# Four graph layers in fp32 on one core: VectorE and block transfers for a transpose, RMS factors by way of DRAM, bias rows on VectorE, five graphs in flight

## The chip, the cores and the metric

The kernel runs on one core of a Trainium2 chip. The time is that of one execution on the device, in microseconds. A core has five engines that work side by side, each through its own queue in order: TensorE (PE: matmuls and transposes, results into PSUM), VectorE (DVE) and ScalarE (ACT) for elementwise work, GpSimd (POOL), and SyncE (SP), which issues the DMA transfers. An instruction that needs another engine's result waits for a semaphore, and all behind it in its queue waits too.

## The reference

There are 32 graphs of 512 nodes with 256 features and a dense 512x512 adjacency matrix each. Four graph layers follow each other, each as `x = layernorm(x + layer(x, adj))`, all in float32:

```python
# layer 0: two-layer perceptron on (1 + eps) x + adj x
h = relu(((1 + eps) * x + adj @ x) @ W1 + b1)           # 256 -> 512
y = h @ W2 + b2                                          # 512 -> 256
# layer 1: linear, aggregate, leaky
y = prelu(adj @ (x @ W.T + b), alpha)
# layer 2: norm, aggregate, two weights, residual
h = layer_norm(x)
y = x + relu((adj @ h) @ W_rel + b_rel + h @ W_root)
# layer 3: aggregate, RMS norm over 1024 hidden features, silu
h = (eps * x + adj @ x) @ W1 + b1                        # 256 -> 1024
h = silu(h * rsqrt(mean(h * h, -1) + 1e-6) * w)
y = h @ W2 + b2                                          # 1024 -> 256
```

## The kernel before

The 32 graphs pass through the core as a pipeline. A graph's nodes are laid over 128 partitions in 4 chunks, so a token-major activation is a tile of 128 x 4 x 256; feature-major ones are 128 features by 512 nodes a chunk. Every matrix product is done by a seven-product scheme on 2x2 blocks (`seven`, with the sums of blocks in `left_sums` and `right_sums`): fewer matmuls on TensorE, more additions on VectorE.

The order of the instructions is worked out in Python while the kernel is built. `Plan` (line 191) records each operation with the engines that may do it (its "ways"), a duration for each way, and what it reads and writes. `Plan.order` (line 317) then goes through a modelled time: each engine takes, among the operations that can start, the one with the best rank, where the rank holds the graph's number times a period plus the time by which TensorE will need the result. `best` (line 311) tries each of `RULES` (line 95) and keeps the order that ends first. A DMA in this model costs SP `ISSUE` = 0.45 us and ends `ADVANCE` + size/385 + `AFTER` later (line 76). What comes out is one fixed sequence for each engine.

Memory is handed out in the same pass. A `Pool` has tiles, a `Room` is one tile's use. There are 36 rooms of 128 x 1024 floats, 12 small tiles and 8 PSUM banks (line 444 and on); at most `FLIGHT` = 4 graphs are open at a time. A younger graph must leave some tiles spare for the older ones.

The parts that the change touches, per graph:

- `Adjacency` (line 634) loads the adjacency in four pieces, forms its block sums (`sums`, line 650), and keeps a plain copy of four diagonal strips (two chunks of 128x128 each) in a room of its own, by four tile-to-tile transfers (`carry`); layer 0 adds (1 + eps) to the diagonals (`with_loops`, line 671), `restore` (line 667) copies the four strips back before layer 1, and layer 3 adds its eps to them.
- `plus_row` (line 874) adds a bias row to a token-major activation in layers 0 and 3: four GpSimd instructions of 128x256.
- `layer2` (line 935) needs its input h feature-major, as hT. For each of two chunks TensorE transposes four squares of 128x128 into a PSUM bank (`flip`), and ScalarE or VectorE copies the bank to a room. Then VectorE forms differences of hT's halves (`dense_sums`), and TensorE multiplies.
- `layer3` (line 955) sums the squares of the hidden features into `acc`; `column_sums` (line 793) adds over the features by a VectorE reduction that transposes 32x32 blocks, three small additions and four small steps `ts` (one for each 32 partitions); GpSimd raises to the power -1/2 (`inv_sqrt`); TensorE spreads the 512 factors over all partitions by four transposes of a broadcast column into a PSUM bank `pr`; VectorE multiplies hT by `pr`, ScalarE applies silu, and the last product follows.
- `load_x` and the output are one transfer each.

Nearly all instructions are recorded through one helper, so the profile shows them under line 266 (compute) and line 280 (DMA). One finds them by the names of their tiles: room (working tiles), ps (PSUM), few (small tiles), ident (the identity for transposes).

Of the kernel before, what the change touches and what calls it, by code (L numbers as in the profile page):

```python
# [26 lines left out]


def in_psum(x):
    return isinstance(x, Part) and x.room.pool.psum  # L30
# [35 lines left out]
def gpsimd_time(n):  # L66
    return 0.15 + n * 0.0024, 0.05


# [6 lines left out]
ISSUE, ADVANCE, AFTER, LANES = 0.45, 1.5, 0.35, 8  # L76
# [18 lines left out]
RULES = [(50, 2, last, near) for last in (12, 20) for near in (0, 0.5, 1)]  # L95


class Pool:


    def __init__(self, tiles, grain, spare, psum):
        self.tiles, self.grain, self.spare, self.psum = tiles, grain, spare, psum
        self.clear()

    def clear(self):
        self.rooms = [None] * len(self.tiles)

    def free(self):

        return sorted(  # L110
            (0.0 if r is None else r.until, i)
            for i, r in enumerate(self.rooms)
            if r is None or not r.left
        )


class Room:


    def __init__(self, pool):  # L120
        self.pool = pool
        self.uses = 0
        self.clear()

    def clear(self):
        self.index = None
        self.left = self.uses
        self.until = 0.0


class Part:
# [34 lines left out]
    def place(self):  # L166
        v = self.room.pool.tiles[self.room.index]
        for step in self.steps:
            v = step(v)
        return v  # L170
# [3 lines left out]
class Op:  # L174

    graph: int
    rank: tuple
    ways: dict  # L180
    port: set
# [9 lines left out]
class Plan:  # L191
# [10 lines left out]
    def grains(self, x):  # L202
        part = isinstance(x, Part)
# [4 lines left out]
        for step, n in dims[:-1]:  # L208
            starts = [s + step * i for s in starts for i in range(n)] if step else starts
        step, n = dims[-1]  # L210
        return {
            (key, g)
            for s in starts
            for g in range(s // grain, (s + step * (n - 1)) // grain + 1)
        }

    def add(self, ways, out, ins, ordered=None, port=(), kbytes=0):
        me = len(self.ops)
        op = Op(self.graph, (self.graph, me), ways, port, "scalar" in ways, kbytes)
        self.ops.append(op)  # L220
        before, results = set(), set()
        writes = self.grains(out) if out is not None else set()
# [22 lines left out]
    def do(self, out, *ways, ordered=None, scrap=None):  # L245
# [3 lines left out]
        port = set()  # L249
        for e, method, _, args, kw in ways:  # L250
            tiles = [x for x in (*args, *kw.values()) if isinstance(x, (bass.AP, Part))]
            ins += tiles
            if e == "gpsimd" and kw.get("op") != ALU.pow or e == "vector" and not (
                method.startswith("bn_") or any(in_psum(x) for x in tiles)
            ):
                port.add(e)

        def issue(engine, method, args, kw):
# [14 lines left out]
            out, ins, ordered, port,  # L273
        )

    def move(self, out, src, kbytes, inward=True):


        def issue():
            self.nc.sync.dma_start(*(x.place() if isinstance(x, Part) else x for x in (out, src)))  # L280

        self.add(
            {"sync": ((ISSUE, ADVANCE + wire_time(kbytes) + AFTER), issue)},
            out if inward else None, [src] if isinstance(src, Part) else [], kbytes=kbytes,
        )
# [31 lines left out]
    def order(self, period, pace, last, near):  # L317
# [15 lines left out]
        oldest, port, wire, lanes = 0, 0.0, 0.0, [0.0] * LANES  # L333
        can_start = {i for i, n in enumerate(behind) if not n}
        done = []
        while can_start:
# [4 lines left out]
            def rooms_free(op):  # L341

                count = {}
                for r in op.rooms:
                    if r.index is None:
                        count[r.pool] = count.get(r.pool, 0) + 1
                at = 0.0
                for pool, n in count.items():
                    if pool not in room_at:
                        room_at[pool] = pool.free()  # L350
                    n += pool.spare[min(op.graph - oldest, len(pool.spare) - 1)]
                    if op.graph - oldest >= self.flight or n > len(room_at[pool]):
                        return None
                    at = max(at, room_at[pool][n - 1][0])
# [3 lines left out]
            for i in can_start:  # L358
# [4 lines left out]
                if op.kbytes:  # L363
                    wait = max(wait, lanes[0])
                at = {
                    e: max(free[e], wait, ready[i][e], port if e in op.port else 0.0)
                    for e in op.ways
                }
                way = min(at, key=lambda e: at[e] + sum(op.ways[e][0]) + (YIELD if op.yields and e == "vector" else 0.0))
# [11 lines left out]
            if op.kbytes:  # L381
                wire = max(wire, t + ADVANCE) + wire_time(op.kbytes)
                end = wire + AFTER
                lanes = [*lanes[1:], end]
            if engine in op.port:
                port = end
            for r in op.rooms:
                if r.index is None:
                    r.index = r.pool.free()[0][1]
                    r.pool.rooms[r.index] = r  # L390
# [16 lines left out]
def tile_gnn_stack(ctx: ExitStack, tc: tile.TileContext, a: dict, out: bass.AP):  # L407
# [36 lines left out]
    FLIGHT, ROOMS, SMALL = 4, 36, 12  # L444
# [3 lines left out]
    psum = ctx.enter_context(tc.tile_pool(name="psum", bufs=1, space=bass.MemoryType.PSUM))  # L448
    plan = Plan(nc, FLIGHT)

    def pool(kind, name, n, size, grain, spare):
        return Pool(
            [kind.tile([P, size], F32, tag=f"{name}{i}", name=f"{name}{i}") for i in range(n)],
            grain, spare, kind is psum,
# [3 lines left out]
    rooms = pool(work, "room", ROOMS, NC * D, P, (0, 4, 6, 8))  # L458
# [5 lines left out]

    def gpsimd(method, n, *args, **kw):
        return "gpsimd", method, gpsimd_time(n), args, kw
# [22 lines left out]
    def both(method, o, x, y, engines):  # L489
        plan.do(o, *(e(method, span(o), x, y) for e in engines))  # L490

    def add(o, x, y, *engines):
        both("tensor_add", o, x, y, engines or (vector,))

    def sub(o, x, y, *engines):
        both("tensor_sub", o, x, y, engines or (vector,))

    def mul(o, x, y):
        both("tensor_mul", o, x, y, (vector,))
# [10 lines left out]
    def carry(o, x):  # L510
        plan.move(o, x, P * span(o) / 256)

    def inv_sqrt(o, x):
        n = span(o)
        plan.do(
            o, ("gpsimd", "tensor_tensor", power_time(n), (x, mhalf[:, 0:n]), dict(op=ALU.pow))
# [3 lines left out]
    def room(*shape):  # L520
        return Part(Room(rooms)).shaped(*shape)

# [54 lines left out]
    mhalf = constant("mhalf", [P, 2 * NC])  # L577
# [56 lines left out]
    class Adjacency:  # L634
# [15 lines left out]
        def sums(self):  # L650
# [8 lines left out]
            kept = room(4, HC, P)  # L659
            self.plain = [kept[:, i] for i in range(4)]  # L660
            for d, o in zip(self.plain, self.loops):
                if plan.graph:
                    carry(d, o)
                else:
                    copy(d, o)

        def restore(self):
            for d, o in zip(self.plain, self.loops):
                carry(o, d)

        def with_loops(self, loop):
            for d, o in zip(self.plain, self.loops):
                add(o, d, loop.unsqueeze(1).to_broadcast(list(o.shape)), vector)

        def row_sums(self):

            rows = room(N)
# [79 lines left out]
    def dense_sums(upper, lower):  # L757
# [3 lines left out]
        for pairs in zip(upper, lower):  # L761
            blocks = [x[:, :, j * TH : (j + 1) * TH] for x in pairs for j in range(2)]
            sums = right_sums(*blocks, [room(2, TH) for _ in range(3)], blocks[1])
# [29 lines left out]
    def column_sums(t, put):  # L793
# [3 lines left out]
        few = small(16)  # L797
# [7 lines left out]
        for q in range(1, P // Q):  # L805
            add(few[0:Q], few[0:Q], few[q * Q : (q + 1) * Q])
        for q in range(P // Q):
            put(slice(q * Q, (q + 1) * Q), few[0:Q, q :: P // Q])
# [64 lines left out]

    def plus_row(x, r):

        for c in range(NC):
            add(x[:, c, :], x[:, c, :], r, gpsimd)
# [31 lines left out]
    def layer1(x, adjacency):  # L909
# [4 lines left out]
        column_sums(rows, lambda p, sums: ts(rs[p], sums, 1.0, None, ALU.mult))  # L914
# [20 lines left out]
    def layer2(h, xx, u, adjacency):  # L935

        aT = aggregate(h, adjacency)
        hT = Wide(DC)
        for j in range(DC):
            ps = bank(N)  # L940
            for c in range(NC):
# [144 lines left out]
```

## Time and profile before

| | us |
|---|---|
| median of 3 runs (2363.84 to 2365.42) | 2364.99 |
| the profiled execution | 2366.02 |
| its span, first to last instruction | 2364.2 |

The mean granted TensorE clock in it was 0.997. In a line of groups stand the source line, engine, operation, tiles written and read, shapes and count, then the busy time in us and the mean of one instruction in ns, then the engine's idle time just before and what ended it. A float32 matmul has two rows on TensorE (MATMUL on PE, its weight load on PEld), a transpose one. What matters for the change, per graph of the 32, from the groups by form:

| what | count a graph | mean of one, ns |
|---|---|---|
| PE transposes of h (ident, room) | 8 | 273 |
| PE transposes of the factors (ident, few) | 4 | 274 |
| ACT copies of hT out of PSUM, 128x512 | 2 | 597 |
| POOL bias adds, 128x256 | 8 | 769 |
| POOL power, 128x4 | 4 | 1243 |
| DVE products of hT with pr, 128x512 | 8 | 679 |
| DMA tile to tile, 128 KB, issue to landing | 8 | 2.2 us |

The durations of PE rows overlap, so the time that one costs is the distance between starts in a row of equal ones. A line of the stretches has its borders, its length, and the busy time and instruction count of PE, PEld, DVE, ACT and POOL, then the granted clock, the share of the DMA engines and their GB/s.

### The profile page before, as it was taken

What the parts mean: (1) busy time and instruction counts of PE and PEld (TensorE: products, weight loads), DVE (VectorE), ACT (ScalarE), POOL (GpSimd) and SP (SyncE); (2) the same over time, 40 slices, a digit from 0 to 9 for tenths busy, and PEclk for the clock granted to TensorE, in tenths of its full rate; (3) what the DMA queues carried; (4) which work ended last, traced back from release to release, by engine and by line L of the source; (5) the groups of instructions that cost most, each with busy time, mean ns of one, the idle gap of its engine ahead of it and who ended that gap; (6) DMA issues with size and microseconds to landing.
All of it is one profiled execution on the core that took longest, in us unless ns stands there. A gap on an engine that the chain in (4) does not pass through costs nothing.

```text
span 2364.2 us, 40948 instructions
## 1 busy us (share of the span) xinstructions
PE 2330.0 (99%) x14362; PEld 2135.4 (90%) x14362; DVE 2138.4 (90%) x5485; ACT 1570.1 (66%) x3994; POOL 407.7 (17%) x422
## 2 busy tenths in 40 slices
PE   8999999999999999999999999999999999989997
PEld 7899989999999999999999999999999989978997
DVE  6899989999999999999999999999999999988997
ACT  3767666667666676766676666776666766565764
POOL 1112111111121121111111211111111112111111
PEclk9999999999999999999999999999999999999999
DMA  7001110111110111101111101111011111011000
GB/s 218 12 8 54 50 54 12 52 50 51 53 35 30 50 54 50 54 14 50 50 52 52 44 20 50 54 50 54 14 50 50 52 52 46 23 52 48 10 10 28
DMA packets 103487, 107.25 MB, mean 45 GB/s; under 512 B 10865, under 2 KB 78193, under 8 KB 103281
## 3 DMA queue, kind: packets, MB, share of 16 engines
q1 hardware_dynamic: 103280, 104.64, 14.5%
q8 instruction: 113, 1.85, 0.3%
q14 instruction: 94, 0.76, 0.1%
HBM read 54.80 MB, written 16.78 MB: 30 GB/s over the span
## 4 chain that ended last, share of the span: by engine, by line
PE 91%; DVE 4%; DMA 2%; ACT 1%; issue 1%; SPq 0%; POOL 0%; POOLq 0%; ACTq 0%; DVEq 0%
PE ps L266 91%; DVE room L266 3%; ACT room L266 1%; DVE few L266 1%; DMA room<-in_x_dram 1%; ACT scrap L266 1%; DMA room<-room 1%; SPq L280 0%; DMA L_gnn_eps<-in_L_gnn_eps_dram 0%; DMA room<-in_adj_dram 0%; POOL few L266 0%; ACT L266 0%; POOLq L1082 0%; DVE L_gnn_W L266 0%; DVE A L266 0%
## 5 line engine op out<-in xcount | busy, mean ns | idle before, releaser
L266 PE MATMUL ps<-room,room 128*128 128x256 f32 x3584 | 911.9, 380 | 9.8 <-DMA room<-in_x_dram 5.8
L266 DVE TENSOR_TENSOR room<-ps,room 128x256 f32<-128x256 f32 (+1 forms) x1344 | 629.6, 475 | 149.3 <-PE ps L266 122.6
L266 PEld LDWEIGHTS ps<-room,room 128*128 128x128 f32 x3584 | 650.1, 191 | 88.8 <-issue 7.1
L266 DVE TENSOR_TENSOR room<-room,room 128x512 f32<-128x512 f32 (+1 forms) x1120 | 640.6, 585 | 9.9 <-ACT room L266 3.1
L266 PE MATMUL ps<-L_gnn_W,room 128*128 128x128 f32 (+1 forms) x3584 | 622.7, 291 | 7.2 <-ACT room L266 4.9
L266 PEld LDWEIGHTS ps<-L_gnn_W,room 128*128 128x128 f32 x3584 | 525.3, 192 | 31.1 <-ACT room L266 7.2
L266 PE MATMUL ps<-A,room 128*128 128x128 f32 x3072 | 489.2, 276 | 1.8 <-ACT room L266 1.1
L266 PEld LDWEIGHTS ps<-A,room 128*128 128x128 f32 x3072 | 434.8, 192 | 15.8 <-ACT room L266 1.3
L266 PE MATMUL ps<-room,L_gnn_W 128*128 128x256 f32 x1536 | 424.6, 380 | 1.0 <-DVE room L266 0.9
L266 ACT ACTIVATE room<-ps,L_gnn_b_c 128x256 f32<-128x256 f32 x768 | 318.2, 472 | 157.2 <-PE ps L266 157.0
L266 POOL TENSOR_TENSOR few<-few,mhalf 128x4 f32<-128x4 f32 (+1 forms) x160 | 212.5, 1329 | 1211.0 <-DVE few L266 1208.5
L266 ACT ACTIVATE room<-ps 128x256 f32<-128x256 f32 (+1 forms) x546 | 215.0, 407 | 298.5 <-PE ps L266 294.7
L266 ACT ACTIVATE room<-room,few 128x256 f32<-128x256 f32 x624 | 341.0, 603 | 107.0 <-DVE few L266 103.7
L266 DVE TENSOR_TENSOR room<-room 128x256 f32<-128x256 f32 (+1 forms) x640 | 330.4, 518 | 18.0 <-DMA room<-in_adj_dram 5.7
L266 POOL TENSOR_TENSOR room<-room,L_gnn_b 128x256 f32<-128x256 f32 x256 | 194.6, 769 | 739.6 <-PE ps L266 519.0
L266 PE MATMUL ps<-room,A 128*128 128x256 f32 x1152 | 319.2, 380 | 3.0 <-ACT room L266 3.0
L266 PEld LDWEIGHTS ps<-room,L_gnn_W 128*128 128x128 f32 x1536 | 279.7, 191 | 33.1 <-DVE room L266 2.2
L266 ACT ACTIVATE room<-room 128x1024 f32<-128x1024 f32 (+2 forms) x260 | 245.8, 946 | 18.1 <-DVE room L266 16.5
L266 ACT ACTIVATE room<-room,L_gnn_rms_weight_c 128x512 f32<-128x512 f32 x256 | 179.7, 718 | 111.3 <-DVE room L266 108.2
L266 PEld LDWEIGHTS ps<-room,A 128*128 128x128 f32 x1152 | 206.5, 191 | 27.1 <-ACT room L266 4.2
L266 ACT ACTIVATE scrap<-room 128x256 f32<-128x256 f32 x384 | 157.2, 411 | 74.3 <-DVE room L266 63.1
L266 ACT ACTIVATE scrap<-room,few 128x256 f32<-128x256 f32 x384 | 190.7, 498 | 18.1 <-DVE few L266 16.3
(53 smaller groups left out, 1453.4 us busy)
## 6 DMA issues: line engine op xcount, KB each, us to landing
room<-in_adj_dram SPq DMA_DIRECT2D x128, 256.0 KB, 5.0
room<-room SPq DMA_DIRECT2D x252, 128.0 KB, 2.2
room<-in_x_dram SPq DMA_DIRECT2D x32, 512.0 KB, 6.0
out_dram<-room SPq DMA_DIRECT2D x32, 512.0 KB, 3.0
L_gnn_W<-in_L_gnn_W_dram SPq DMA_DIRECT2D x2, 1024.0 KB, 8.5
L_gnn_W<-in_L_gnn_W_dram SPq DMA_DIRECT2D x2, 512.0 KB, 8.1
L_gnn_b<-in_L_gnn_b_dram SPq DMA_DIRECT2D x3, 128.0 KB, 5.0
L_gnn_W_rel<-in_L_gnn_W_rel_dram SPq DMA_DIRECT2D x1, 256.0 KB, 7.2
```

Source lines behind the costliest of these rows:

```text
L266: getattr(getattr(self.nc, engine), method)(to, *(put(x) for x in args), **kw)
```

## The change

- hT in layer 2: VectorE transposes each chunk within squares of 32x32 into another room, and 16 tile-to-tile transfers put the squares into their places (for each pair of 32-partition groups, 8 pieces of 32 numbers on 32 partitions).
- The RMS factors in layer 3: one small step on 32 partitions in place of four, the power on 32x16, a write of the 512 numbers to a line in DRAM, and a read of that line by all partitions into half a room. The product reads that room and no PSUM bank.
- The first and the last graph (`alone()`) keep TensorE's transposes for both.
- `plus_row`: two VectorE instructions of 128x512 in place of four on GpSimd.
- Diagonals: two of the four strips are kept in DRAM, not in a room; the other two are restored from the input adjacency in four pieces. The diagonal additions are done in place.
- A room can be used in halves (`short`), for `acc`, the row sums, some block sums and the factors.
- Five graphs in flight in place of four, 11 small tiles, other spare counts and other rules for the planner; the planner no longer models the memory port that GpSimd and VectorE share. Dependences are told apart by 32-partition groups.

```diff
-ISSUE, ADVANCE, AFTER, LANES = 0.45, 1.5, 0.35, 8
+ISSUE, ADVANCE, AFTER, LANES = dict(sync=0.45, gpsimd=1.2), 1.5, 0.35, 8
...
-RULES = [(50, 2, last, near) for last in (12, 20) for near in (0, 0.5, 1)]
+RULES = [(p, c, last, near) for p, c in ((36, 2), (45, 2.5)) for last in (12, 20) for near in (0.25, 0.5)]
...
-    FLIGHT, ROOMS, SMALL = 4, 36, 12
+    FLIGHT, ROOMS, SMALL = 5, 36, 11
...
+    memory = ctx.enter_context(tc.tile_pool(name="memory", bufs=1, space=bass.MemoryType.DRAM))
+    lines = cycle([memory.tile([N], F32, tag=f"line{i}", name=f"line{i}") for i in range(FLIGHT)])
+    diagonals = cycle(
+        [
+            memory.tile([P, 2, 2, P], F32, tag=f"diagonal{i}", name=f"diagonal{i}")
+            for i in range(FLIGHT)
+        ]
+    )
+    def alone():
+        return plan.graph in (0, B - 1)
...
-    rooms = pool(work, "room", ROOMS, NC * D, P, (0, 4, 6, 8))
+    rooms = pool(work, "room", ROOMS, NC * D, P, (0, 2, 4, 4))
...
+    def short(*shape):
+        return Part(Room(rooms, whole=False)).shaped(*shape)
...
-            kept = room(4, HC, P)
-            self.plain = [kept[:, i] for i in range(4)]
-            for d, o in zip(self.plain, self.loops):
-                if plan.graph:
-                    carry(d, o)
...
+            if plan.graph:
+                self.kept = next(diagonals)
+                for i in (2, 3):
+                    d = self.kept[:, i - 2]
+                    name = f"{self.kept.tensor.name}{i}"
+                    plan.move(d, self.loops[i], P * HC * P / 256, into=name)
...
         def restore(self):
-            for d, o in zip(self.plain, self.loops):
-                carry(o, d)
+            for i in range(4):
+                if plan.graph == 0:
+                    carry(self.loops[i], self.kept[:, i])
+                elif i < 2:
+                    for k in range(HC):
+                        c = i * HC + k
+                        block = a["adj"][plan.graph][:, c, c * P : (c + 1) * P]
+                        plan.move(self.loops[i][:, k], block, P * P / 256)
                 else:
+                    name = f"{self.kept.tensor.name}{i}"
+                    d = self.kept[:, i - 2]
+                    plan.move(self.loops[i], d, P * HC * P / 256, outof=[name])
...
+    def turned(h):
+        hT = Wide(DC)
+        if alone():
+            for k in range(DC):
+                ps = bank(N)
+                for c in range(NC):
+                    flip(ps[:, c * P : (c + 1) * P], h[:, c, k * P : (k + 1) * P])
+                copy(hT.chunk(k), ps)
+        else:
+            squares = Wide(DC)
+            for k in range(DC):
+                o = squares.chunk(k)
+                plan.do(o, vector("transpose", N, h[:, :, k * P : (k + 1) * P]))
+            places = [slice(q * Q, (q + 1) * Q) for q in range(P // Q)]
+            to, of = (
+                x.pair(0).then(lambda v: v.rearrange("p k (c i) -> p (k c) i", i=P))
+                for x in (hT, squares)
+            )
+            for p in places:
+                for q in places:
+                    carry(to[p, :, q], of[q, :, p])
+        return hT
+
+    def everywhere(sums, ops):
+        if alone():
...
+        else:
+            few = small(2, N // Q)
+            ve, power = few[0:Q, 0, :], few[0:Q, 1, :]
+            ts(ve, sums, *ops)
+            inv_sqrt(power, ve)
+            o, line = short(N), next(lines)
+            plan.move(line.rearrange("(m i) -> i m", i=Q), power, N / 256, into=line.tensor.name)
+            plan.move(o, line.partition_broadcast(P), P * N / 256, outof=[line.tensor.name])
+        return o
...
     def plus_row(x, r):
-        for c in range(NC):
-            add(x[:, c, :], x[:, c, :], r, gpsimd)
+        for h in range(2):
+            add(half(x, h), half(x, h), r.unsqueeze(1).to_broadcast([P, HC, D]))
...
-        hT = Wide(DC)
-        for j in range(DC):
-            ps = bank(N)
-            for c in range(NC):
-                flip(ps[:, c * P : (c + 1) * P], h[:, c, j * P : (j + 1) * P])
-            copy(hT.chunk(j), ps)
+        hT = turned(h)
...
-        hT, acc = Wide(FC3), room(N)
+        hT, acc = Wide(FC3), short(N)
...
-        pr = bank(N)
-        for c in range(NC):
-            flip(pr[:, c * P : (c + 1) * P], rstd[:, c : c + 1].spread(P, P))
+        pr = everywhere(column_sums(acc), (1.0 / HID3, RMS_EPS, ALU.mult, ALU.add))
```

## The prediction, made before the change was run

> **What bounds the kernel now.** I read the busy shares of the page first, then the chain of waits, the busy time by stretches, and the timeline of one graph.
>
> ```profile
> PE 2330.0 (99%) x14362; PEld 2135.4 (90%) x14362; DVE 2138.4 (90%) x5485; ACT 1570.1 (66%) x3994; POOL 407.7 (17%) x422
> ...
> PE 91%; DVE 4%; DMA 2%; ACT 1%; issue 1%; SPq 0%; POOL 0%; POOLq 0%; ACTq 0%; DVEq 0%
> ```
>
> TensorE (PE) holds the chain, and VectorE (DVE) is close behind. The stretches show where TensorE rests:
>
> ```profile
> 0.00:75.00 75.00, 63.75 (x316) 54.14 (x317) 56.34 (x154) 33.93 (x89) 9.16 (x16) 0.98 0.58 176
> ...
> 600.00:1200.00 600.00, 600.00 (x3695) 551.73 (x3694) 551.16 (x1417) 408.46 (x1043) 107.92 (x110) 1.00 0.14 43
> ...
> 1800.00:2200.00 400.00, 391.34 (x2382) 355.56 (x2381) 351.35 (x912) 257.24 (x678) 70.12 (x74) 1.00 0.14 42
> ...
> 2300.00:2364.00 64.00, 51.57 (x359) 48.24 (x357) 50.65 (x129) 30.56 (x56) 9.07 (x10) 0.93 0.06 25
> ```
>
> In the middle TensorE has no idle time. It loses 11.3 us at the start, 8.7 between 1800 and 2200, 12.4 at the end. A busy TensorE needn't be at its rate, so I count its rows. From the timeline of TensorE (start, length, group):
>
> ```profile
> 630.31 0.49 PE L266 MATMUL ps<-ident,room 128*128 128x128 f32 x3
> 635.52 0.60 PE L266 MATMUL ps<-ident,few 128*128 128x128 f32 x4
> ...
> 1011.06 1.28 PE L266 MATMUL ps<-L_gnn_W,room 128*128 128x128 f32 x10
> ...
> 1021.08 1.46 PE L266 MATMUL ps<-room,room 128*128 128x256 f32 x6
> ```
>
> Spacing inside a group is (length - one duration)/(count - 1): (1.28-0.276)/9 = 0.1116 us for a row of 128 columns, (1.46-0.380)/5 = 0.216 for 256 columns, (0.49-0.273)/2 = 0.109 for a transpose. A matmul here is two rows, a transpose one. The groups by form hold, per graph, 212 rows of 256, 224 of 128 and 12 transposes: 45.8 + 25.0 + 1.3 = 72.1 us. The same GpSimd (POOL) step of two graphs lies 72.09 us apart:
>
> ```profile
> 614.40 1.12 POOL L266 TENSOR_TENSOR few<-few,mhalf 128x4 f32<-128x4 f32 x1 [1.68 <-DVE few L266]
> ...
> 686.49 1.12 POOL L266 TENSOR_TENSOR few<-few,mhalf 128x4 f32<-128x4 f32 x1 [1.68 <-DVE few L266]
> ```
>
> So the steady state is TensorE's instruction count and nothing else. But it is timed closely: if each matmul's start is set against the release it waits for (semaphore events, 400 to 1800 us), the median margin is 0.5 us behind ScalarE and 0.75 behind VectorE. Any wait that makes VectorE late by more than this reaches TensorE.
>
> **What the Trainium skill says.** "VectorE: DVE Perf Modes", section "The three transpose paths": VectorE transposes within 32x32 blocks only; hence the 16 transfers that move the blocks. No run here shows the plain form, but a reduction with a transpose is in the trace. "SBUF — State Buffer", section "Who interferes with whom": a VectorE instruction with two SBUF inputs and a GpSimd one that reads SBUF exclude each other. The trace fits without proving it: a pair of bias adds on GpSimd takes anything from 1.45 to 1.87 us. "DMA: Bandwidth & Descriptors", section "Anatomy of one DMA": about 2 us fixed, most of it the receipt of the write, longest for HBM. Here a tile-to-tile transfer lands in 2.2 us; an output of 512 KB in 2.6 to 3.0. The same page's "Rules for kernel authors": a last dimension that is not contiguous becomes one descriptor per element; the column loads at the start (4-byte packets) agree.
>
> **The change, part by part.** The profiled execution is 2366.02 us, span 2364.2 plus 1.8 around it; the median of the runs is 2364.99, 1.0 below.
>
> *TensorE.* In graphs 1 to 30 all 12 transposes go (8 for hT, 4 for the RMS factors), 360 in the program's order: 360 x 0.109 = 39.2 us, all on the bounding engine. A graph's need falls to 70.8 us.
>
> *ScalarE* loses two 128x512 evictions a graph (597 ns each) and takes no such work; at 66% busy this is worth nothing.
>
> *VectorE.* Counts by spacing (0.60 us for 512 elements, 0.33 for 256, 0.07 for small ones): its need is about 60 us a graph now, the rest of the 66 busy being overlapping tails and waits. Added: two transposes, four bias adds of 512 elements (two calls, two halves each); no row shows the plain transpose, the nearest is the reduction with a transpose,
>
> ```profile
> L266 DVE TRANSPOSE_TENSOR_REDUCE few<-room 128x16 f32<-128x512 f32 x64 | 45.2, 707 | 0.9
> L266 DVE TENSOR_TENSOR room<-room,room 128x512 f32<-128x512 f32 x672 | 464.2, 696 | 6.6 <-DMA room<-in_adj_dram 2.7 <-ACT room L266 1.8
> ```
>
> so 0.60 by spacing; 1.2 if it ran at half rate, 0.5 at the least. 6 x 0.60 = 3.6. Four small factor steps become one (-0.2), and the new order gives VectorE some 1.6 more normalisation pieces a graph (+0.5). In all about 64 of 70.8 us. It stays below TensorE, also at 1.2 (65). The eight GpSimd adds (8 x 0.77 = 6.2 us a graph) that could shut it out are gone.
>
> *Transfers.* SyncE (SP) issues 32 DMAs a graph instead of 14; SP has room (32 x 0.65 = 21 us of 71), but its queue is in order, and 16 stand in a row behind the wait for the transposes. The changed order has 22 to 25 VectorE instructions, 9.6 us by spacing, between the second transpose and the first VectorE instruction that reads hT (a difference of its halves). TensorE reads hT much later; the reader that counts is VectorE, because everything behind it, evictions that TensorE waits for among them, stands in the same queue. The transfers need 15 steps of issue plus one landing:
>
> ```profile
> L280 SPq DMA_DIRECT2D room<-room x252: 593/594/688, 13.7 to 2204.2; - x126
> L280 SPq DMA_DIRECT2D room<-in_adj_dram x128: 327/441/2332, 0.7 to 2175.2; - x128
> ```
>
> At the step of a plain row (0.441 + 0.04) the last lands 0.2 + 7.2 + 2.2 = 9.6 us after the transpose: just covered. At that of the present tile-to-tile form (0.594 + 0.05) it is 0.2 + 9.7 + 2.2 = 12.1: VectorE stands 2 to 2.5 us. The new shape (32 partitions, 8 pieces of 128 bytes) is neither. I take 0.53 us, 10.3 in all, 0.7 late, of which the 0.5 us margin takes most: 0.3 us a graph.
>
> *RMS factors.* On the new path stand one small step, the power on 32x16 (1243 ns for 4 columns, 1672 for 8, so 107 ns a column: 2.5), the write of 512 four-byte pieces, and the read back by all partitions. Bounds for the write: 2.2 (tile-to-tile) and 4; I take 2.6, as the smallest output landing. For the read: 2.2, and 5.0, the median of adjacency loads in a burst; 2.9. With hand-overs 0.1 + 2.5 + 2.6 + 2.9 + 0.3 = 8.4, against 26 to 28 VectorE instructions (8.1 to 8.3 us by spacing) between the small step and the first product. Late by 0 to 3; I take 0.3 for TensorE.
>
> *The rest.* Diagonals kept in DRAM and restored from there: 0.5 to 1 us later than now, with the next aggregation some instructions away; nothing. In-place diagonal adds: same count, nothing. SP's diagonal copies were the first to wait for an adjacency load; in the new order VectorE's differences are. That is 0 to 1 us a graph; I take nothing, since the loads go out in pairs there and not in a burst. Five graphs in flight and half rooms: the drain holds 8.7 + 12.4 us of idle TensorE now; a fifth graph can fill some of it, but the last graph still ends alone. Between 0 and -20; I take -8.
>
> Sum: 2366.0 - 39.2 + 28 steady graphs x 0.6 (16.8) - 8 = 2335.6: **2336 us**.
>
> **The rivals.**
>
> *The 16 transfers set the pace (slower).* Place: the first VectorE reader of hT. Price at 0.645 us a step: 2.3 us late, less 0.5 of margin, 1.8 x 28 = 50 us; with 0.3 x 28 of the factors, 2366 - 39 + 50 + 8 - 8 = 2377, and 2400 if the factors' path is also 1 us late. It decides against the change from a step of about 0.6 us on. For it: 0.594 is the steadiest row of SP's list, with as many descriptors (256). Against: a fourth of the bytes and of the partitions, and 4-byte column loads of two and four pieces were issued in 379 and 470 ns.
>
> *All of it is hidden.* The step is 0.48 or less, the drain fills: 2366 - 39 - 18 = 2309. For it: SP, DMA (14.5% of 16 engines) and GpSimd have time. Against: the margins of 0.5 us.
>
> *VectorE becomes the bound.* It was busy 551.2 of 600 us, 66.2 a graph; if those tails don't shrink, 66.2 + 3.9 = 70.1 of 70.8, and the two queues wait on each other in turn. The gain is then half eaten or all: 2350 to 2368. For it: the 92%. Against: 60 by spacing, and fewer exclusions with GpSimd.
>
> That the change doesn't do what it says is out: the order has the 360 transposes gone, 480 block transfers, 30 line writes and 30 reads.
>
> **How the numbers follow.** Forecast (2322 to 2350): 0.36. Hidden: 0.14. VectorE bound: 0.12, of which half is within 0.2% (4.7 us, what a measurement of this kernel tells from no change). Transfers: 0.38, from 2366 up. Faster: 0.36 + 0.14 + 0.03 = 0.53, trimmed to 0.51 for what I can't see; within 0.2%: 0.07; slower: 0.42. For 8 in 10 the range goes from 2306 to 2398; the forecast's own is 2322 to 2350.
>
> **What would show it.** Transposes of hT near 0.69 us long; VectorE's idle time before an instruction that reads room, released by a DMA room<-room, near 0.7 us a graph if right, over 2 if the rival holds; SP's row for that form near 500 ns or near 600; TensorE's period 71.4 us a graph (70.8 hidden, over 72.1 for the rival). Wrong is the whole reading if TensorE waits in the middle for something else than VectorE or ScalarE, or if VectorE is busy without pause.

## The result, and the profile after

The changed kernel takes **2681.03 us** (median of 4 runs, 2678.76 to 2683.10) against 2364.76 us for the kernel before beside it: 1.1338 times as long, with a 95% interval of 1.1318 to 1.1357. The forecast was 2336 (2306 to 2398). The profiled execution is 2679.07 us, its span 2677.2 with a mean granted TensorE clock of 0.953 (before: 0.997).

The page of the changed kernel, with the parts that answer to the busy shares, the chain and the list of DMA issues (size of one, median us from issue to landing):

```profile
PE 2392.9 (89%) x14002; PEld 2150.2 (80%) x14002; DVE 2198.5 (82%) x5606; ACT 1515.5 (57%) x3911; POOL 331.0 (12%) x166
...
PE ps L283 4%; DVE room L283 2%; DMA line<-few 1%; DMA room<-line 1%; POOL few L283 1%; ACT room L283 0%; DVE few L283 0%; POOLq L1168 0%; ACTq L1168 0%; SPq L298 0%; DVEq L283 0%; ACTq L283 0%
...
room<-in_adj_dram SPq DMA_DIRECT2D x128, 256.0 KB, 4.8
...
room<-room SPq DMA_DIRECT2D x480, 32.0 KB, 1.9
...
room<-line SPq DMA_DIRECT2D x30, 256.0 KB, 3.6
```

TensorE's 360 matmul records less are there (14362 - 14002), but its idle time is 2677.2 - 2392.9 = 284 us where it was 34. (A row is one record on PE. Every row has a weight load on PEld beside it, also a transpose, so both counts are the same; the two rows of a float32 matmul are two records on PE.) The chain of this page covers only a tenth of the span, so it can't be asked for the bound; the waits can. The same stretch of the middle as before (columns as there: the engines' busy time, then the clock, the DMA share and GB/s):

```profile
600.00:1200.00 600.00, 529.02 (x3086) 476.84 (x3086) 483.59 (x1237) 331.09 (x857) 78.60 (x35) 0.94 0.17 44
```

Before, all 600 us were busy, at a clock of 1.00. Now 71 are idle, and the mean clock is 0.94. From one write of a line to the next graph's, a graph takes 84.3 us (mean of 17 between 500 and 2000 us), where it took 72.1. The waits of the changed kernel by engine (who waits, for whom: us in total, times, longest):

```profile
DVE room L283 <- DMA room<-line: 203.4, 30, 8.9
...
DVE room L283 <- DMA room<-room: 62.7, 26, 4.1
...
DVE room L283 <- DMA room<-in_adj_dram: 8.8, 4, 3.9
...
PEld ps L283 <- ACT room L283: 192.6, 54, 9.4
...
SPq L298 <- DMA line<-few: 193.7, 30, 8.0
```

VectorE stands for the spread RMS factors in every one of 30 graphs, 6.8 us on average, and 26 times for hT, 2.4 us on average. Three engines then wait in a row: SyncE for the line to be written, VectorE for it to be read back, TensorE (by way of ScalarE) for VectorE. The timeline of one such place, engine by engine; first VectorE, GpSimd, SyncE, then TensorE (start, length, group, idle time before it and what ended that):

```profile
1060.22 0.22 DVE L283 TENSOR_SCALAR few<-few 32x16 f32<-32x16 f32 x2
...
1069.63 0.40 DVE L283 TENSOR_TENSOR room<-room 128x256 f32<-128x256 f32 x1
1076.88 1.29 DVE L283 TENSOR_TENSOR room<-room,room 128x512 f32<-128x512 f32 x2 [6.84 <-DMA room<-line]
...
1060.45 7.00 POOL L283 TENSOR_TENSOR few<-few,mhalf 32x16 f32<-32x16 f32 x2 [5.20 <-DVE few L283]
...
1066.51 0.33 SPq L298 DMA_DIRECT2D line<-few  x1
1073.20 0.33 SPq L298 DMA_DIRECT2D room<-line  x1
...
1071.33 0.59 PE L283 MATMUL ps<-room,room 128*128 128x256 f32 x2
1078.38 0.80 PE L283 MATMUL ps<-L_gnn_W,room 128*128 128x128 f32 x2 [6.46 <-ACT room L283]
1078.97 1.06 PE L283 MATMUL ps<-room,room 128*128 128x256 f32 x2
1079.83 1.06 PE L283 MATMUL ps<-L_gnn_W,room 128*128 128x256 f32 x2
1080.68 1.06 PE L283 MATMUL ps<-room,room 128*128 128x256 f32 x2
...
1082.10 1.03 PE L283 MATMUL ps<-room,room 128*128 128x256 f32 x4
```

The path can be read off it. The small step ends at 1060.44; the power runs to just before SyncE's write at 1066.51 (6.0 us; the GpSimd group also holds a 128x4 power behind it); the write lands when the read is issued, at 1073.20 (6.7); the read lets VectorE go at 1076.88 (3.7). That is 16.4 us. VectorE came to the first product after 9.6, and 1.0 of these it had waited for the second power, which stood behind the long one. TensorE runs 0.59 us for two rows of 256 before its pause of 6.46 us and 1.06 after it. The starts 1078.97, 1079.83, 1080.68 lie 0.427 us a row apart, twice the 0.216 of before; from 1082.10 on the rate is full again. So each such pause costs its own length, and the work of the next 3.5 us or so then takes twice as long.

The trace also records the granted clock itself. In the changed kernel it stood at one half for 253 us in all, in 38 stretches of 3.4, 6.8 or 10.2 us. TensorE was idle for 97 of these us and busy for 155. Half of the busy part, 78 us, is work lost; before it was 3. So the clock's whole shortfall, (1 - 0.953) x 2677.2 = 126 us, is not all lost work. With all 28 pauses over 3.4 us, and with 9 of the 11 between 2.0 and 3.4 us, such a stretch begins in the pause or at most 3.5 us after it.

The account of 2677.2 - 2364.2 = 313 us: TensorE's idle time grew by 250; its busy time by 63, which is 39 less for the transposes and 102 more. Of the 102 some 75 (78 - 3) are the half clock; the rest is not assigned. It needs no lower clock: the kernel with both parts undone, below, has as many rows as the kernel before and a clock of 0.998, and is busy 18 us longer (2348.1 against 2330.0).

### The profile page after: what moved, and what is told of

Read it like the earlier page. It is cut to its first block, busy times and chain, and to the rows that moved or that the text cites. A ratio compares the mean times of both kernels' runs of the same rounds, so it can differ in the third digit from the quotient of the medians.

```text
span 2677.2 us, 40587 instructions
## 1 busy us (share of the span) xinstructions
PE 2392.9 (89%) x14002; PEld 2150.2 (80%) x14002; DVE 2198.5 (82%) x5606; ACT 1515.5 (57%) x3911; POOL 331.0 (12%) x166
## 2 busy tenths in 40 slices
DMA packets 238335, 122.80 MB, mean 46 GB/s; under 512 B 157745, under 2 KB 209201, under 8 KB 238129
## 5 line engine op out<-in xcount | busy, mean ns | idle before, releaser
L283 PE MATMUL ps<-room,room 128*128 128x256 f32 x3584 | 979.6, 392 | 14.0 <-DVE room L283 7.8
L283 DVE TENSOR_TENSOR room<-room,room 128x512 f32<-128x512 f32 (+1 forms) x1360 | 776.6, 594 | 207.8 <-DMA room<-line 203.4
L283 PE MATMUL ps<-L_gnn_W,room 128*128 128x128 f32 (+1 forms) x3584 | 666.6, 301 | 194.8 <-ACT room L283 168.5
L283 PEld LDWEIGHTS ps<-L_gnn_W,room 128*128 128x128 f32 x3584 | 591.6, 199 | 265.0 <-ACT room L283 178.1
L283 DVE TENSOR_TENSOR room<-ps,room 128x256 f32<-128x256 f32 (+1 forms) x1344 | 611.0, 471 | 96.5 <-PE ps L283 91.3
L283 POOL TENSOR_TENSOR few<-few,mhalf 128x4 f32<-128x4 f32 (+2 forms) x160 | 330.3, 2068 | 2340.5 <-DVE few L283 1722.3
L283 ACT ACTIVATE room<-room,few 128x256 f32<-128x256 f32 x573 | 305.7, 594 | 157.7 <-DVE few L283 156.6
L283 DVE TENSOR_TENSOR room<-room 128x256 f32<-128x256 f32 (+1 forms) x640 | 311.9, 496 | 98.6 <-DMA room<-room 62.7
L283 ACT ACTIVATE room<-ps 128x256 f32<-128x256 f32 (+1 forms) x514 | 190.2, 377 | 251.4 <-PE ps L283 249.5
L283 DVE TENSOR_TENSOR room<-room,loop 128x256 f32<-128x256 f32 x256 | 106.1, 416 | 21.4 <-PE ps L283 14.8
```

The source lines that it names most:

```text
L283: getattr(getattr(self.nc, engine), method)(to, *(put(x) for x in args), **kw)
```

## The experiments

Each was timed beside the kernel before on its own chip (2365.2 to 2365.8 us). The ratios are to that.

### Which part costs what: the factors, hT, both by TensorE again

Three kernels, each the changed one with one condition always true (`everywhere` in e1_factors_pe, `turned` in e2_hT_pe, both in e3_both_pe), so that the old way is taken in every graph:

```diff
     def everywhere(sums, ops):
-        if alone():
+        if True:
```

> The changed kernel with one part undone: the RMS factors are spread by TensorE in every graph, as before; all else stays. Theory A (VectorE waits for the factors' way through DRAM: 203 us of its idle time, 30 times, and TensorE stands behind it and then runs at half clock): the 203 us and most of the half-clock time go, 2677 - 203 - some 80 of clock + 120 x 0.109 = about 2410, between 2370 and 2450. Theory B (the 16 transfers of hT set the pace): little changes, over 2600. Theory C (VectorE has too much work with the bias rows and transposes): little changes, over 2600.

> The changed kernel with the other part undone: hT comes from TensorE's transposes in every graph; the factors still go through DRAM. Theory A: only the 63 us that VectorE waits for tile-to-tile transfers go, and their share of the clock, against 26 us of transposes that come back: about 2620, between 2580 and 2660. Theory B: under 2450. Theory C: 2650 or more.

> Both undone: what is left of the change is the bias rows on VectorE, the diagonals by way of DRAM, half rooms and five graphs in flight. Theory A with B for the rest: the kernel is TensorE's count again, 2350 to 2370, no different from before by more than 1%. Theory C: VectorE's idle time is gone and TensorE waits for it, over 2400.

| factors by | hT by | us | ratio (95%) | clock |
|---|---|---|---|---|
| DRAM | transfers (the change) | 2681.0 | 1.1338 (1.1318 to 1.1357) | 0.953 |
| DRAM | TensorE (e2) | 2570.3 | 1.0866 (1.0850 to 1.0882) | 0.969 |
| TensorE (e1) | transfers | 2445.2 | 1.0340 (1.0322 to 1.0359) | 0.991 |
| TensorE | TensorE (e3) | 2396.7 | 1.0136 (1.0112 to 1.0160) | 0.998 |

The first lies in the range of its theory A. The second is 10 us below its own, and the third fits none of its theories: it is above the 2370 of A and below the 2400 of C. The factors' path costs 174 us where hT is by TensorE and 236 where it isn't; the transfers cost 48 or 111. Even with both undone some 31 us stay. The planner makes a new order for every kernel, so these are sizes and no exact parts. With the factors by TensorE the wait for hT is what is left, in the list of VectorE's waits of that kernel:

```profile
DVE room L283 <- DMA room<-room: 53.5, 18, 5.7
```

### The same operations, awaited later

The planner's prices for the new operations were set to what the trace shows; what is computed, and by which instructions, stays. Only the order is made anew from these prices (e4_true_costs).

```diff
-    return 0.37 + n * 0.158, 0.04
+    return (0.37 + n * 0.158 if n <= 8 else 6.0), 0.04
...
-                    carry(to[p, :, q], of[q, :, p])
+                    plan.move(to[p, :, q], of[q, :, p], Q * 2 * N / P * Q / 256, issue_time=0.65)
...
-            plan.move(line.rearrange("(m i) -> i m", i=Q), power, N / 256, into=line.tensor.name)
-            plan.move(o, line.partition_broadcast(P), P * N / 256, outof=[line.tensor.name])
+            plan.move(line.rearrange("(m i) -> i m", i=Q), power, N / 256, into=line.tensor.name, late=5.2)
+            plan.move(o, line.partition_broadcast(P), P * N / 256, outof=[line.tensor.name], late=1.2)
```

> All operations of the change stay; only the planner's prices are set to what the trace of the changed kernel shows: 0.65 us for an issue of a block transfer in place of 0.45, 6.0 us for the power on 32x16 in place of 2.9, 5.2 us more for the write of the line to land, 1.2 more for its read. If the loss is one of order alone (nothing is too slow, it is only awaited too early), five graphs hide the path of 17 us and TensorE is the bound with 360 transposes less: 2310 to 2350. If the path through DRAM costs time however early it is issued (rooms and queues held), it stays over 2400.

**2356.61 us** (2354.5 to 2361.9), ratio 0.9967 (0.9954 to 0.9980): 324 us less than the changed kernel, and 0.33% below the kernel before. It was the fastest of all. The time came out some 7 us above the forecast for "order alone", but the sign and nearly the whole size are those of that theory. The write and the transfers are as slow as ever (the write lands after 7.0 us in the median, 6.7 in the change): from its timeline, one line's write and read on SyncE, 6.5 us apart, and one row of 16 transfers:

```profile
895.94 10.80 SPq L299 DMA_DIRECT2D room<-room  x16
...
926.01 0.42 SPq L299 DMA_DIRECT2D line<-few  x1
932.54 0.33 SPq L299 DMA_DIRECT2D room<-line  x1
```

But VectorE has other work until the factors are there. In its timeline the small step stands at 922.37 and the first product at 941.22, with no wait for the line ahead of it: 18.7 us after the step's end, where the change had 9.6. One thing got shorter with the order: the power takes 3.3 us in the median, where the change had 5.0 and the new price says 6.0. At this place the write goes out 3.5 us after the step, where it was 6.0, so the path is 2.5 us shorter here; that alone would not have covered a wait of 6.8.

```profile
922.37 0.16 DVE L284 TENSOR_SCALAR few<-few 32x16 f32<-32x16 f32 x1
...
940.63 0.67 DVE L284 SCALAR_TENSOR_TENSOR room<-room,room 128x512 f32<-128x512 f32 x1
941.22 1.29 DVE L284 TENSOR_TENSOR room<-room,room 128x512 f32<-128x512 f32 x2
```

The stretch of the middle:

```profile
600.00:1200.00 600.00, 597.66 (x3646) 545.88 (x3645) 565.77 (x1451) 391.34 (x1011) 79.54 (x42) 1.00 0.19 51
```

TensorE is busy again, at the full clock. VectorE is at 94%.

### Each price alone

Two kernels, each with half of these edits: only the factors' three prices (e6_factor_prices), or only the 0.65 us an issue for hT (e7_issue_price).

> As e4_true_costs, but only the factors' path is priced as the trace has it; the hT transfers keep 0.45 us an issue where they take 0.65. If each wait is a matter of its own price, the wait for the line stays away and the one for hT comes back with about 2.4 us a graph: 2390 to 2430. If the factors' price was all, as e4: 2350 to 2362.

> The reverse: the hT transfers are priced at 0.65 us an issue, the factors as in the changed kernel. If the prices are separate, VectorE no longer waits for hT but still about 6 us a graph for the line, with the half clock after it: 2570 to 2640, near e2's 2570. If the new order happens to cover the factors too, under 2450.

With the factors' prices alone 2389.07 us (ratio 1.0101, 1.0086 to 1.0116), with the issue price alone 2615.66 (1.1052, 1.1036 to 1.1069). The first is a shade below its range of 2390 to 2430. The factors' prices take away the factors' wait: of the two waits VectorE keeps only the one for hT, 34.8 us in all. With the issue price alone the wait for the line stays, 196.9 us in 30 waits, and hT's wait falls to half (62.7 to 32.1) without going, while VectorE's wait for adjacency loads grows from 8.8 to 34.5. So most of the loss hangs on the factors' prices.

### Why the write is so slow: longer pieces

The line in DRAM is laid out as the power has it, so that each of 32 partitions writes one piece of 64 bytes, where there were 512 pieces of 4 bytes. The product reads the spread factors through a strided view. The instructions stand in the same order on every engine as in the changed kernel (e5_long_pieces).

```diff
-            plan.move(line.rearrange("(m i) -> i m", i=Q), power, N / 256, into=line.tensor.name)
+            plan.move(line.rearrange("(i m) -> i m", i=Q), power, N / 256, into=line.tensor.name)
...
+            o = o.then(lambda v: v.rearrange("p (i m) -> p m i", i=Q))
...
-                mul(hT.chunk(f), hT.chunk(f), pr)
+                y = hT.chunk(f).then(lambda v: v.rearrange("p (m i) -> p m i", i=Q))
+                mul(y, y, pr)
```

> The changed kernel in its own order of instructions, but the line in DRAM is laid out as the power has it (32 partitions, one piece of 64 bytes each, in place of 512 pieces of 4 bytes); the product reads the spread factors through a strided view. If the 4-byte pieces make the write land 6.7 us after its issue, it lands in 2 to 2.6 us, VectorE's wait for the line falls from 6.8 to about 2.5 us a graph, TensorE's idle time is then too short for the half clock, and the kernel takes 2470 to 2560 us. If the landing is the price of any write to DRAM just ahead of a read, nothing moves: 2670 to 2690. If the strided view costs VectorE, its products show it as longer than 0.70 us.

2552.78 us (2551.42 to 2553.09), ratio 1.0791 (1.0773 to 1.0809), clock 0.990. The write lands 1.31 to 1.34 us after its issue in the stretch looked at (600 to 900 us), where the changed kernel's takes 6.5 to 7.2. So the small pieces made the landing, and not the DRAM or the read behind it. The pages count the pieces: 223935 DMA packets here against 238335, 14400 less, which is 30 x (512 - 32). The wait for the line falls from 203.4 us to

```profile
DVE room L283 <- DMA room<-line: 38.9, 25, 2.7
```

The time fell by 128 us only, though the wait for the line fell by 164.5. The groups by form show a likely reason, each kernel's line of the form that holds the products (mean ns is the second number after the bar). In the changed kernel

```profile
L283 DVE TENSOR_TENSOR room<-room,room 128x512 f32<-128x512 f32 x912 | 607.5, 683 | 207.3 <-DMA room<-line 203.4 <-DMA room<-in_adj_dram 2.0
```

and with the longer pieces

```profile
L283 DVE TENSOR_TENSOR room<-room,room 128x512 f32<-128x512 f32 x912 | 691.5, 775 | 42.7 <-DMA room<-line 38.9 <-DMA room<-in_adj_dram 1.9
```

The group grew by 84 us. 240 of its 912 are products that read through the view, so each of these is 0.35 us longer (1.03 in place of 0.68): the strided read cost VectorE 84 us. That this held the time up is not shown by itself; the next kernel drops the stride, but it also has a new order. The half clock is not gone either: 13 stretches of it remain, though no pause of TensorE is longer than 3.43 us.

### Long pieces and no stride

One VectorE transpose of 32x32 turns the factors before the write; 16 partitions then write 128 bytes each, in the order of the nodes, and no reader is strided. One kernel has this with the change's own prices (e10_rows), the other with those of the kernel with true prices, but for the line (the write 0.5 us below its plain price, the read 0.6 above; e9_rows_true_costs).

```diff
-            few = small(2, N // Q)
-            ve, power = few[0:Q, 0, :], few[0:Q, 1, :]
-            ts(ve, sums, *ops)
-            inv_sqrt(power, ve)
+            few = small(2, Q)
+            twice, turn = few[0:Q, 0], few[0:Q, 1]
+            ts(
+                twice.then(lambda v: v.rearrange("p (t m) -> p t m", t=2)),
+                sums.then(lambda v: v.unsqueeze(1).to_broadcast([Q, 2, N // Q])), *ops
+            )
+            inv_sqrt(twice[:, 0 : N // Q], twice[:, 0 : N // Q])
+            plan.do(turn, vector("transpose", Q, twice))
+            power = turn[0 : N // Q]
...
-            plan.move(line.rearrange("(m i) -> i m", i=Q), power, N / 256, into=line.tensor.name)
+            plan.move(line.rearrange("(m i) -> m i", i=Q), power, N / 256, into=line.tensor.name)
```

> The changed kernel with its own prices, with the same small transpose and 128-byte pieces. Its order is made anew, so it is no exact neighbour. The path is then about 0.1 + 5 + 0.1 + 1.3 + 3.1 us = 9.6 against a window of some 8.2: VectorE waits 1 to 2 us a graph for the line and 2 for hT, without e5's strided product (8 x 0.35 us a graph): 2440 to 2500. If e5's loss was not the stride, it stays at 2540 to 2560.

> As e4_true_costs, with one small VectorE transpose of the factors (32x32) ahead of the write, so that the line leaves from 16 partitions in pieces of 128 bytes and no reader is strided; the planner has the write at its plain price less 0.5 us and the read at 0.6 more. If the write's landing falls to about 1.3 us as in e5 and the shorter path frees rooms and order: 2335 to 2352, below e4's 2356.6. If e4 had hidden the path already and other waits set the rest: 2352 to 2362.

With the change's prices 2442.45 us (ratio 1.0315, 1.0286 to 1.0344): at the low end of its range, and without the 1 to 2 us a graph for the line that it allowed for: that wait all but goes (0.9 us in all), since the power also got shorter in this order (median 2.89 us), and the one for hT stays (65.8). With true prices it is 2370.60 (ratio 1.0027, 1.0017 to 1.0037), above both of its ranges and slower than the kernel with slow writes and true prices. No wait for a transfer is large in its trace (3.6 us in all for the line, 8.8 for hT). VectorE waits 67.4 us in all for TensorE, where the kernel with slow writes has 51.1, and TensorE is idle 48 us against 43 and busy 8 us longer, in many small places. So this miss isn't explained. Two orders that the planner thinks sound differed by 14 us here, and the shorter path brought no gain where the longer one was covered.

### What made the 31 us that stayed

Three attempts on the kernel with both undone. First the bias rows back on GpSimd (e8_both_pe_bias_pool), then four graphs in flight with the old rules (e11_both_pe_four). The edit of the first:

```diff
-            add(half(x, h), half(x, h), r.unsqueeze(1).to_broadcast([P, HC, D]))
+            for c in (2 * h, 2 * h + 1):
+                plan.do(x[:, c, :], ("gpsimd", "tensor_add", (0.764, 0.05), (x[:, c, :], r), {}))
```

> As e3_both_pe (hT and factors by TensorE, 2396.7), with the bias rows back on GpSimd in quarters. If the bias rows on VectorE make e3's 31 us over the kernel before, they go: 2360 to 2375. If it is the order with five graphs in flight, half rooms or the diagonals in DRAM, it stays: 2385 to 2405.

> As e3_both_pe (hT and factors by TensorE), with four graphs in flight and the planner's rules of the kernel before. If e3's 31 us over the kernel before come from the order that five graphs and the new rules give: 2362 to 2380. If they come from what stays (the diagonals by way of DRAM, the bias rows on VectorE): 2388 to 2405.

The bias rows on GpSimd gave 2427.72 us (ratio 1.0262, 1.0247 to 1.0278), slower by another 31 and outside both ranges; four graphs and the old rules 2406.50 (1.0173, 1.0158 to 1.0189), 1.5 above the range for "what stays". So taking back the bias rows, or the five graphs and the new rules, each in an order made anew, did not take the loss away. Then prices again: 1.5 us more for an adjacency load, 0.5 for a power (e12_both_pe_priced).

```diff
-    return 0.37 + n * 0.158, 0.04
+    return 0.87 + n * 0.158, 0.04
...
-            plan.move(chunk, a["adj"][b][:, m, :], P * N / 256)
+            plan.move(chunk, a["adj"][b][:, m, :], P * N / 256, late=1.5)
```

> As e3_both_pe (hT and factors by TensorE, 2396.7), with two prices set nearer to the trace: an adjacency load 1.5 us later (in e3 VectorE waits 28 times for one, 33.9 us in all), a power 0.5 us longer (TensorE waits some 43 us for powers there). If e3's 31 us over the kernel before are such waits, they go, and with them most of the loss: 2362 to 2380. If they are the added work on VectorE or the diagonals' way through DRAM, the waits go but the time stays: 2385 to 2400.

2371.94 us (2371.34 to 2373.67), ratio 1.0028 (1.0017 to 1.0039): 25 of the 31 us are gone. VectorE's wait for adjacency loads, with both undone and the change's prices,

```profile
DVE room L283 <- DMA room<-in_adj_dram: 33.9, 28, 3.9
```

and with the two prices mended,

```profile
DVE room L284 <- DMA room<-in_adj_dram: 6.8, 6, 4.0
```

and the weight loads' waits for a power fall from 26.4 us to 0.2. This kernel keeps the bias rows on VectorE, the diagonals by way of DRAM and the five graphs, so these are not what cost the 25. How the 25 divide between the two prices was not tried, nor were the diagonals kept in rooms.

## Why the prediction was wrong

**TensorE.** 360 transposes less is right. What they are worth alone was not measured. The floor of 70.8 us a graph was not reached: in the kernel with true prices TensorE's rate between 400 and 2000 us is 9710 records in 1600 us against 9924, so with 436 rows a graph in place of 448 the period is 71.8 us where it was 72.2. Of 1.3 us taken away, 0.4 came out. Its idle time there is only 0.3 us a graph; why the rest did not come out is open.

**The factors: the step that failed.** "Late by 0 to 3; I take 0.3" is the line of the sum that broke. Measured, VectorE was late by 6.8 us a graph, and two terms of the path account for it. The write was bounded by 2.2 and 4 us, taken at 2.6, from transfers of long rows; it landed in 6.1 to 8.4 (the middle half of the 30 in 6.5 to 7.2). I had named what the Trainium skill says of such writes, "DMA: Bandwidth & Descriptors", "Rules for kernel authors", one descriptor an element, and then priced it by rows that hadn't that. It was the term with no like in the trace, and its upper bound should have been open. The power was carried on from 4 and 8 columns to 2.5 us; at the least it takes 2.89, and in this order 5.0 in the median, up to 6.4. It lies beside VectorE's additions. The groups have its mean:

```profile
L283 POOL TENSOR_TENSOR few<-few,mhalf 32x16 f32<-32x16 f32 x30 | 154.2, 5141 | 214.4 <-DVE few L283 214.4
```

Over the 30 of them the length goes with the time that VectorE instructions with two SBUF inputs overlap it (correlation 0.94): 2.89 us for the one with none, 6.03 in the median of the 23 with more than 4 us. This fits what the Trainium skill says in "SBUF — State Buffer", "Who interferes with whom": a VectorE instruction with two SBUF inputs contends with a GpSimd one that reads SBUF. It is no proof. A longer power overlaps more in any case, and in the kernel with pieces of 128 bytes and the change's prices (e10_rows) most powers lie beside some 2.3 us of such instructions and still take 2.89 in the median. No run tried it by itself. The prediction used the section for the GpSimd adds that went, and not for the power that came. The read, 2.9 taken and 3.6 measured, was within its bounds.

**The window is no slack.** The prediction set a path of 8.4 us against a window of 8.1 to 8.3 as if the two were independent. Measured at the place above, the path was 16.4 and the window 9.6. The two aren't independent. The planner puts the first product where its own prices say that the factors will have landed; from the code, 2.9 for the power, 1.5 + 0.35 for the write, 1.5 + 0.66 + 0.35 for the read, and four hand-overs of 0.13 to 0.2 come to 8.0. So an error of a price comes out as a wait. The kernel with true prices shows it: there the prices add up to some 17 us (6.0 + 7.05 + 3.7 and the hand-overs), the window is 18.7, and the kernel takes 324 us less.

**hT.** The step of 0.53 us, taken between 0.48 and 0.645, was 0.65: the rival's value. SyncE's list for the changed kernel (ns, shortest, median, longest):

```profile
L298 SPq DMA_DIRECT2D room<-room x484: 585/609/2050, 14.5 to 2508.3; - x162
```

A quarter of the bytes and partitions saved nothing against the 0.594 of the old form, which spoke for the rival and was set aside. Its lateness of 2.3 us a graph was measured as 2.4 in 26 waits. Its 50 us were too few: with the factors by TensorE the transfers make the kernel 48 us slower although 240 transposes are gone, which are 26 us at 0.109 each. By this estimate they cost some 74, VectorE's transposes among it. That rival had its mechanism right, and gave only 2377 for the whole because it too took the factors as nearly covered.

**What a wait costs.** Both the forecast and the rivals passed lateness on at most one to one. TensorE ran at half rate for about 3.5 us after a long pause, which no rival had: some 75 us of the loss. The Trainium skill has it, "TensorE: Matmul & The Clock Gate", "HAM oscillation — how this bites in real kernels": no idle gap of TensorE above about 3.4 us. For long pauses the trace agrees: a pause of 6.46 us, then 0.427 us a row. But 3.4 us is no safe limit here: 9 of the 11 pauses between 2.0 and 3.4 us had a stretch of half clock too, and with the longer pieces 10 of 22. Where the wait for the line was 1.6 us on average (38.9 / 25), the clock was 0.990.

**The rest.** The VectorE transpose took 688 ns, as foreseen (0.69). VectorE is busy 82%, so it was no bound in the change; in the kernel with true prices it is at 94% and the time, 2356.6, lies in the range of the rival "VectorE becomes the bound", but whether it is that was not tried. "The loads go out in pairs" was wrong: the four large ones go within 3 us (1035.99 to 1038.46 with the x load) and land after 4.8 in the median. That cost the change nothing to speak of: VectorE waits 8.8 us for them, and 8.3 in the kernel before,

```profile
DVE room L266 <- DMA room<-in_adj_dram: 8.3, 6, 4.0
```

but 33.9 in the kernel with both undone. The gain of 8 at the ends isn't to be seen in the changed kernel; with true prices TensorE is idle 26 us at the start (to 75 us), between 2000 and 2200 and from 2300 to the end, where the kernel before had 32. But from 75 to 400 us it is idle 9.5 us where it was 1.7, and over the whole span 43 where it was 34, so on balance no idle time was filled.

## What to carry to other kernels

Where a planner or a hand-made order places a consumer at the moment its own price list says the data will be there, there is little slack to hide an error in: before a new operation goes in, measure it in its place, and put that number in the list. In the fastest kernel here one price was too long (6.0 us for a power that took 3.3); the prices that were too short became waits. Price a wait of the bounding engine by its length and by what it does to that engine's clock. And a transfer of many tiny pieces wants a price of its own, however few bytes it moves.

## What the runs showed of the hardware

- A write of 2 KB from SBUF to DRAM landed 6.1 to 8.4 us after its issue as 512 pieces of 4 bytes and in 1.3 (median) as 32 pieces of 64; its issue took 0.33 us on SyncE either way.
- A tile-to-tile transfer of 32 partitions in 8 pieces of 128 bytes was issued in 0.609 us, one of 128 partitions in two pieces of 512 bytes in 0.594 (both medians): 256 pieces each, and four times the bytes made the issue no longer.
- A VectorE product of 128x512 whose second input has a stride of 64 bytes took 1.03 us against 0.68.
- TensorE's clock stood at one half in stretches of 3.4, 6.8 or 10.2 us. With all 28 pauses over 3.4 us of the changed kernel, with 9 of the 11 between 2.0 and 3.4 us, and with 1 of the 22 between 1 and 2 us, such a stretch began in the pause or at most 3.5 us after it.
